# Another order inside the last attention layer, and additions of gathered rows placed one at a time

## The chip, the cores and the metric

The kernel runs on one core of a Trainium2 chip. The metric is device time in microseconds (us) of one execution, the median of several runs. Everything is float32.

## What is computed

The input is x of shape (8, 256, 32, 32): eight items, each with 256 channels and 1024 tokens. There are two layers. The first is attention with 8 heads of 64 whose softmax runs over the query axis. The second normalises the tokens, does attention without heads, whose keys and values are the normalised tokens themselves, adds it to its input, normalises again and adds a mixture of experts: 8 experts, of which every token uses the best two.

```python
def _L1_attn_ref(x, W):
    xa = jnp.einsum('bnd,ed->bne', x, W)
    scores = jnp.einsum('bne,bme->bnm', xa, x)
    attn = jax.nn.softmax(scores, axis=-1)
    return jnp.einsum('bnm,bmd->bnd', attn, x)

# _L1_ffn_ref: logits = tokens @ router_w.T; the two largest of 8; combine = their
# normalised weights;  out = tokens + sum over e of
#     combine[:, e:e+1] * (gelu(tokens @ w1[e] + b1[e], approximate=False) @ w2[e] + b2[e])

x = _L0_conv_ref(x, w_qkv, b_qkv, w_out, b_out)          # layer 0
t = _to_tokens(x)
t = t + _L1_attn_ref(_ln_t(t), L1_attn_W)                # attend
t = t + _L1_ffn_ref(_ln_t(t), router_w, w1, b1, w2, b2)  # norm 2, experts
x = _from_tokens(t, x)
```

## The kernel before

The items are worked one after the other. For each of items 0 to 6 the kernel does layer 0 (`layer0`, lines 465 to 676), the attention of layer 1 (`attend`, line 678), the second norm and the router's logits (`normed`, line 996), stores the tokens with their norm added (`sums`), and sends every token's row to the lists of its two experts (`dispatch`). Matmuls of the next item's values (`pv`, line 408) are placed as filling into `attend` by the calls `fill(place)`. After layer 0 of item 7, `experts` (line 1226) works through the lists of items 0 to 6 in blocks of 256 rows and writes the results to `y` in the chip's memory. Last come `attend` and `dense` (line 1458) for item 7: `dense` does all 8 experts for all tokens of item 7, in 16 half steps (expert e, half n) of 512 tokens. In the same time the class `Results` (line 1336) finishes items 0 to 6.

**Attention of layer 1.** The normalised tokens are transposed (`pt_n`, line 281), multiplied by W (`px`, line 708), and the scores come from a scheme of seven products on sums of halves instead of eight. One `Pair` k makes two blocks of 128 queries: products into the banks x and v of one `ps1` tile and into `ps1z` (line 761). ACT copies x away after the first, the s2 and the s3 product (lines 744, 754 and 756), and VectorE adds the other banks to these copies and takes the row's minimum on the way (`nlow`, line 771). `rest` adds two last products, finds the maximum, and ACT takes the exponential (lines 795, 804, 812). A block of weights must then be turned before its product with the values (`mix`: the eight matmuls of one `py` group, line 861, and the eviction t, line 870). Blocks 0 and 7 are turned by TensorE (`turn_now`, tile `pa`). Blocks 1 to 6 are turned by VectorE in squares of 32 (`turn`, line 833), and their 16 pieces are then moved by ACT copies and by transfers of SP's queue, half and half (line 844; both appear in the profile as spare<-home, aT<-home or home<-home). The program's order is written out by hand, in the last lines of `attend`, and with `tc.issue_after`, which places an instruction behind another on its engine. PSUM has three two-bank tiles (`big`: ps1, pa, px, pt_n) and two one-bank tiles (`acc`: ps1z, py, pdy).

**Results.** A unit is a block of 128 tokens of one item; there are 56. For a unit, POOL gathers the two rows of every token from `y` (`yk`, line 1391: two gathers of 128 KB), and VectorE adds them, with their weights, to the item's sums `o` (line 1413: two instructions). SP loads one item's sums ahead (1 MB, `load`). When an item's eight units are done, it is stored in two halves: VectorE transposes a half (`oT`, line 1449), and SP sends four transfers of 128 KB (line 1456). The calls `tick(place, instruction)` in `attend` and `dense` look the place up in the table `PLACES`, which says how many units are added behind that instruction, how many are gathered and how many halves are stored. The gathered rows have eight slots.

**Dense stage.** A half step has `hidden` (eight matmuls `pdh`, line 1518, and the activation on ACT) and `collect` (two `pdy` banks of eight matmuls each, line 1542, each emptied by two VectorE instructions, line 1551). `hidden` of one half step is issued ahead of `collect` of the one before. `tick(("dense", k), ...)` comes once for each half step, after its second bank.

**Last norm.** For item 7 the second norm of blocks 0 to 6 is done ahead of the last `py` group (`fill("last products")`), that of block 7 after it; all write one tile `n2`. POOL adds the norm to the tokens in one instruction (line 1008).

## Time and profile before

| | us |
|---|---|
| median of three runs (lowest, highest) | 2337.22 (2333.23, 2338.61) |
| the profiled execution: own time | 2328.95 |
| the profiled execution: span | 2327.1 |
| attention of item 6, first transpose to last py (next item's values in it) | 71.8 |
| attention of item 7, the same | 86.9 |
| end of it to the router's first matmul | 10.4 |
| from there to the end of TensorE's work | 125.6 |
| from there to the end of the span | 7.3 |

The profile shows one execution. Its time and its span differ by 1.9 us, which lie around the span. A row of a stretch or a group gives busy time, the number of instructions in brackets, and for groups the mean duration of one and the idle time of the engine before them, with what ended it. In a list of waits, the numbers are the total, how many times, and the longest.

### The profile page before, as it was taken

To read this page: it belongs to the slowest core of one execution; us is meant where nothing else is said; L and a number is where in the kernel's file an instruction comes from. 1 tells how busy PE (TensorE), PEld (TensorE's weight loads), DVE (VectorE), ACT (ScalarE), POOL (GpSimd) and SP (SyncE) were. 2 spreads that over 40 slices of the span, in tenths; PEclk is the share of its full clock that TensorE was granted. 3 is DMA by queue.
4 is the path that set the end of the run, shared out by engine and by line. 5 is a ranking of instruction groups with operands and counts; after the bars stand their busy time and mean duration, and the time that the engine had idled before them with its cause. 6 is when DMAs were issued, how large, how long until landed. Compare 5 with 4: busy or idle time off the path is not lost.

```text
span 2327.1 us, 37989 instructions
## 1 busy us (share of the span) xinstructions
PE 2261.6 (97%) x13059; PEld 1216.1 (52%) x13059; DVE 1554.5 (67%) x4029; ACT 1163.0 (50%) x2138; POOL 410.7 (18%) x392
## 2 busy tenths in 40 slices
PE   9999999999999999999999999999999999998798
PEld 3345533563456335643564355435553488884565
DVE  5775687567855786578657775777568766436655
ACT  3664466456635663656365646465646622225211
POOL 0000012000200020003000200020002135545563
PEclk9999999999999999999999999999999999999899
DMA  8995201020103010201020101100111157765574
GB/s 294 385 386 154 68 17 39 9 56 13 44 2 62 8 49 1 46 19 53 3 46 19 49 8 29 36 26 13 23 42 42 49 145 192 192 199 145 154 210 113
DMA packets 278759, 200.10 MB, mean 86 GB/s; under 512 B 189576, under 2 KB 232232, under 8 KB 276776
## 3 DMA queue, kind: packets, MB, share of 16 engines
q1 hardware_dynamic: 252472, 139.14, 21.2%
q0 software_dynamic: 25008, 58.01, 7.8%
q8 instruction: 104, 1.70, 0.3%
q10 hardware_dynamic: 1088, 0.52, 0.1%
q14 instruction: 87, 0.71, 0.1%
HBM read 108.88 MB, written 110.90 MB: 94 GB/s over the span
## 4 chain that ended last, share of the span: by engine, by line
PE 80%; ACT 5%; DVE 4%; issue 4%; DMA 3%; POOL 3%; SPq 1%; another core or an unknown queue 0%; DVEq 0%; ACTq 0%; POOLq 0%
PE po L569 19%; PE psc L492 19%; PE py L861 7%; PE pqk L371 7%; PE pr L671 5%; PE pv L408 4%; PE ps L761 4%; PE ph L1269 3%; PE pe L1295 3%; PE px L708 2%; POOL yk L1391 2%; PE pqk L349 2%; PE ps1z L761 2%; DMA y<-yb 1%; ACT aT L844 1%
## 5 line engine op out<-in xcount | busy, mean ns | idle before, releaser
L533 ACT ACTIVATE ex<-psc,nmax 128x1024 f32<-128x1024 f32 x512 | 570.0, 1114 | 299.8 <-DVE scrap L516 217.4
L492 PE MATMUL psc<-qk,qk 64*64 64x512 f32 x4096 | 575.8, 593 | 3.8 <-ACT ex L533 3.5
L569 PE MATMUL po<-ex,vs 64*64 64x512 f32 x4096 | 570.6, 591 | 3.6 <-DVE vs L549 2.6
L516 DVE TENSOR_SCALAR_CACHE_REDUCE scrap<-psc,nmax 128x512 f32<-128x512 f32 x512 | 384.2, 750 | 160.3 <-PE psc L492 133.6
L507 DVE TENSOR_REDUCE nmax<-psc 128x1 f32<-128x512 f32 x512 | 350.1, 684 | 9.3 <-PE psc L492 9.3
L492 PEld LDWEIGHTS psc<-qk,qk 64*64 64x64 f32 x4096 | 180.4, 132 | 279.2 <-ACT ex L533 132.6
L569 PEld LDWEIGHTS po<-ex,vs 64*64 64x64 f32 x4096 | 176.5, 132 | 275.6 <-DVE vs L549 82.1
L1081 POOL DMA_INDIRECT rows<-n,d_at x112 | 109.0, 973 | 661.1 <-DVE nmax L507 660.8
L1008 POOL TENSOR_TENSOR t<-t,n 128x2048 f32<-128x2048 f32 x8 | 36.3, 4535 | 875.5 <-DVE n L263 875.5
L371 PE MATMUL pqk<-xT,wqkv 128*128 128x512 f32 x384 | 171.2, 599 | 0.0
L861 PE MATMUL py<-n,spare 128*128 128x256 f32 x512 | 122.0, 394 | 11.3 <-DMA out_dram<-oT 3.8
L336 ACT ACTIVATE qk<-pqk,b_qks 128x512 f32<-128x512 f32 x124 | 85.6, 690 | 86.7 <-PE pqk L371 77.6
L1391 POOL DMA_INDIRECT yk<-y,yat x112 | 111.3, 994 | 76.4 <-issue 28.4
L371 PEld LDWEIGHTS pqk<-xT,wqkv 128*128 128x128 f32 x384 | 71.0, 190 | 99.9 <-issue 77.0
L408 PE MATMUL pv<-wqkv,xT 128*128 128x512 f32 x256 | 121.5, 599 | 1.5 <-DVE v L416 1.0
L861 PEld LDWEIGHTS py<-n,spare 128*128 128x128 f32 x512 | 100.7, 198 | 38.1 <-issue 23.9
L671 PE MATMUL pr<-wo,res 128*128 128x256 f32 x512 | 111.9, 379 | 0.7 <-ACT res L588 0.7
L844 ACT COPY spare<-home 32x256 f32<-32x256 f32 x256 | 103.0, 402 | 10.0 <-DVE home L833 6.7
L671 PEld LDWEIGHTS pr<-wo,res 128*128 128x128 f32 x512 | 97.2, 190 | 17.7 <-ACT res L588 4.7
L1279 ACT ACTIVATE hb<-ph,wb 128x256 f32<-128x256 f32 x96 | 40.1, 470 | 126.9 <-issue 89.4
L533 ACT ACTIVATION_READ_ACCUMULATOR ex<-psc,nmax 128x1 f32 x512 | 99.1, 194 | 0.0
L870 DVE SCALAR_TENSOR_TENSOR t<-py,rs,t 128x256 f32<-128x256 f32 x64 | 30.5, 476 | 98.0 <-PE py L861 85.3
(256 smaller groups left out, 2939.7 us busy)
## 6 DMA issues: line engine op xcount, KB each, us to landing
rows<-wb SPq DMA_DIRECT2D x7, 8192.0 KB
xr<-rows SPq DMA_DIRECT2D x252, 64.0 KB
y<-yb POOLq DMA_DIRECT2D x63, 256.0 KB
xs<-in_x_dram SPq DMA_DIRECT2D x64, 128.0 KB
spare<-home SPq DMA_DIRECT2D x256, 32.0 KB
out_dram<-oT SPq DMA_DIRECT2D x60, 128.0 KB
xT<-in_x_dram SPq DMA_DIRECT2D x7, 1024.0 KB
sums<-t SPq DMA_DIRECT2D x7, 1024.0 KB
```

The source lines that it names most:

```text
L371: mm = nc.tensor.matmul(pq[:, ts(n, 512)], wqkv[:, cc, t, ts(g, P)], xT[:, cc, ts(n, 512)], start=(cc == 0), stop=(cc == NCC - 1),)
L408: nc.tensor.matmul(pv, self.xT[:, cc, ts(i, P)], wqkv[:, cc, 2, :], start=(cc == 0), stop=(cc == NCC - 1),)
L492: mm = nc.tensor.matmul(pss[at, h][ts(c, DK), ts(n, 512)], k[r, j * P + c * DK : j * P + (c + 1) * DK], q[r, ts(n, 512)], start=True, stop ...
L507: firsts[at, h] = nc.vector.tensor_reduce(nmax, pss[at, h][:, ts(0, 512)], AX.X, ALU.max, negate=True)
L516: seconds[h] = nc.vector.tensor_scalar(scrap, pss[at, h][:, ts(1, 512)], -1.0, nmaxes[at, h], ALU.mult, ALU.min, accum_out=nmax,)
L533: nc.scalar.activation(ex, pss.pop((at, h)), AF.Exp, bias=nmaxes.pop((at, h)), scale=1.0, accum_out=sums[at][:, h : h + 1],)
L569: mm = nc.tensor.matmul(po[n][ts(h, DK), :], vss[at][keys, h, :], exps[at, h][keys, ts(n, 512)], start=(j == 0 and turn == 0), stop=(j == ...
L671: nc.tensor.matmul(pr[:, :C], res[:, g, ts(i, P)], wo[:, g, :], start=(g == 0), stop=(g == NPAIR - 1))
L761: return nc.tensor.matmul(to, stationary[:, ts(self.k, P)], moving, start=start, stop=True, skip_group_check=not start,)
L844: move(to[ts(k, SQ), a], since[ts(a, SQ), k])
L861: evicted["mixed"] = nc.tensor.matmul(py[:, :D], aT[m], n1[:, m, :], start=(m == 0), stop=(m == NT - 1))
L1391: ins = nc.gpsimd.indirect_dma_start(out=self.slot(at)[:, k, :], out_offset=None, in_=self.group.y[:, :], in_offset=bass.IndirectOffsetOnAxis(
```

## The change

It has five parts.

- **Order of the attention, for all items.** `Pair.middle` is split: `middle` has the s2 product, `end` has the s3 product. In pair 2 the value projection (`fill("between")`) stands between them, in pair 3 the product py of block 2's weights (`mix(*third)`). `fill("last products")` no longer issues a value projection, so their number stays the same. In pair 3 the ACT copy of the first product and the product into `ps1z` are issued in a separate step (`open`), after pair 2's copies of turned pieces. The exponential of block 2 is issued later (`soften`), behind the first copy of pair 2.
- **The last transposition.** Of block 6's 16 pieces, ACT copies 10 and SP transfers 6.
- **Where rows are added.** `PLACES` puts 14 units into the attention of item 7 and 42 into the dense stage, three for each half step: one behind the first bank's eviction, two behind the second's. Before, 22 were in the attention (three behind most py evictions), 3 at the gates and 31 in the dense stage. All stores of items 0 to 6 now stand in the dense stage, one half of an item for each half step; four of them were in the attention. Each gather follows an addition.
- **Twelve slots.** Eight as before, and four in the buffers of the experts' rows (`xr`). Twelve units are gathered at the start of item 7's attention, two before.
- **Last norm of item 7 in two tiles.** Blocks 0 to 6 and block 7 have tiles of their own, and POOL's addition becomes two.

```diff
...
 
         return t.unsqueeze(2).to_broadcast([P, NT, n])
 
+    class Split:
+
+        def __init__(self, first, last):
+            self.first, self.last = first, last
+
+        def __getitem__(self, key):
+            p, i, c = key
+            return self.first[p, i, c] if i < NT - 1 else self.last[p, 0, c]
+
     class Norm:
 
 
...
             elif place == "norm 2":
                 with tc.issue_after(evicted["mixed"].ins):
                     self.project(True)
-            self.values(1)
+            if place != "last products":
+                self.values(1)
 
         def all(self):
             for _ in range(3):
...
             def __init__(self, k):
                 self.k = k
                 both = big(f"ps1_{b}_{k}")
-                self.x, v = both[:, :HALF], both[:, HALF:]
-                self.z = acc(f"ps1z_{b}_{k}")
+                self.x, self.v = both[:, :HALF], both[:, HALF:]
                 self.ex = [homes[EX[2 * k + h]] for h in range(2)]
                 self.low = [
                     small.tile([P, 1], F32, tag=f"nlow{h}", name=f"nlow_{b}_{k}_{h}")
...
                 ]
                 self.left = self.ex[0][:, :HALF]
                 self.product(self.x, a11, b11, True)
+                if k < 3:
+                    self.open()
+                else:
+                    self.product(self.v, a12, b21, True)
+
+            def open(self):
                 self.first = nc.scalar.copy(self.left, self.x)
-                second = self.product(v, a12, b21, True)
-                tc.declare_no_dep(second.ins, self.first.ins, reason="the other bank")
+                if self.k < 3:
+                    second = self.product(self.v, a12, b21, True)
+                    tc.declare_no_dep(second.ins, self.first.ins, reason="the other bank")
+                self.z = acc(f"ps1z_{b}_{self.k}")
                 self.product(self.z, s1_, t1_, True)
-                self.add(self.left, v, 3.0e38, self.low[0])
+                self.add(self.left, self.v, 3.0e38, self.low[0])
 
             def middle(self, behind=None):
+                with tc.issue_after(behind.ins) if behind else nullcontext():
+                    mm = self.product(self.x, s2_, t2_, False)
+                self.second = nc.scalar.copy(self.ex[0][:, HALF:], self.x)
+                return mm
+
+            def end(self):
                 far = self.ex[1][:, HALF:]
-                with tc.issue_after(behind.ins) if behind else nullcontext():
-                    self.product(self.x, s2_, t2_, False)
-                self.second = nc.scalar.copy(self.ex[0][:, HALF:], self.x)
                 self.product(self.x, s3_, t3_, False)
                 self.third = nc.scalar.copy(far, self.x)
-                self.add(far, self.z, 3.0e38, self.low[1])
+                tick(("low", self.k), self.add(far, self.z, 3.0e38, self.low[1]))
                 return self
 
             def product(self, to, stationary, moving, start):
...
 
                 def even():
                     tick(("max", 2 * k), self.add(ex0[:, HALF:], self.z, self.low[0], nmax[0]))
+                    if k != 1:
+                        self.soften()
+
+                def soften():
                     with tc.issue_after(behind.ins) if behind else nullcontext():
                         nc.scalar.activation(
                             ex0, ex0, AF.Exp, bias=nmax[0], scale=-1.0, accum_out=ssum[0][:, 0:1]
                         )
 
+                self.soften = soften
                 def odd():
                     last = nc.vector.tensor_scalar(
                         scrap, self.x, -1.0, self.low[1], ALU.mult, ALU.min, accum_out=nmax[1]
...
 
             at_sq, at_aT = SQ_AT[i]
             sq = homes[at_sq]
-            nc.vector.transpose(sq, ex)
+            tick(("squares", i), nc.vector.transpose(sq, ex))
             if at_aT is None:
                 aT = two.tile([P, S], F32, tag="tr", name=f"aT_{b}_{i}")
             else:
...
             since = sq.rearrange("p (m k q) -> p k m q", k=NQ, q=SQ)
             for a in range(NQ):
                 for k in range(NQ):
-                    move = nc.sync.dma_start if (a + k) % 2 else nc.scalar.copy
+                    away = (a + k) % 2 and (i < 6 or a > 0)
+                    move = nc.sync.dma_start if away else nc.scalar.copy
                     with tc.issue_after(behind[a * 2 // NQ].ins) if behind else nullcontext():
                         move(to[ts(k, SQ), a], since[ts(a, SQ), k])
             return [aT[:, ts(m, P)] for m in range(NT)]
...
             for m in range(NT):
                 nc.tensor.transpose(pt[:, ts(m, P)], ex[:, ts(m, P)], ident)
             aT = two.tile([P, S], F32, tag="tr", name=f"aT_{b}_{i}")
-            nc.vector.tensor_copy(aT, pt)
+            tick(("now", i), nc.vector.tensor_copy(aT, pt))
             return [aT[:, ts(m, P)] for m in range(NT)]
 
         def mix(at, aT, ssum, more):
...
         def turned(at, ex, ssum, more, behind=None):
             return at, turn(at, ex, behind), ssum, more
 
-        pairs = [Pair(0).middle(), Pair(1).middle()]
+        pairs = [Pair(0)]
+        pairs[0].middle()
+        pairs[0].end()
+        pairs.append(Pair(1))
+        pairs[1].middle()
+        pairs[1].end()
         first, second = pairs[0].rest(pairs[1].third)
         second = turned(*second)
         third, fourth = pairs[1].rest()
         now = turn_now(0, first[1])
         pairs.append(Pair(2))
+        pairs[1].soften()
+        pairs.append(Pair(3))
         mix(0, now, *first[2:])
-        pairs[2].middle(evicted["mixed"])
+        between = pairs[2].middle(evicted["mixed"])
+        with tc.issue_after(between.ins):
+            fill("between")
+        pairs[2].end()
         third = turned(*third, (pairs[2].first, pairs[2].second))
         fourth = turned(*fourth, (pairs[2].second, pairs[2].second))
         mix(*second)
         fifth, sixth = pairs[2].rest()
-        pairs.append(Pair(3))
-        mix(*third)
-        pairs[3].middle()
+        pairs[3].open()
+        between = pairs[3].middle()
+        with tc.issue_after(between.ins):
+            mix(*third)
+        pairs[3].end()
         fifth = turned(*fifth, (pairs[3].second, pairs[3].second))
         sixth = turned(*sixth, (pairs[3].third, pairs[3].third))
         mix(*fourth)
...
             tick("normed", layer_norm(t2, n2, 1e-5, f"f{b}"))
         else:
             n2 = norm.dst
-            tick("normed", norm.blocks(NT - 1, NT))
+            written = norm.blocks(NT - 1, NT)
+            tick("normed", written)
         fill("norm 2")
         nT = one.tile([P, NCC, S], F32, tag="nT", name=f"n2T_{b}")
         tick("turned", to_channels(n2, nT, f"n2_{b}"))
 
-        nc.gpsimd.tensor_add(t2, t2, n2)
+        if norm is None:
+            nc.gpsimd.tensor_add(t2, t2, n2)
+        else:
+            for part, at in ((n2.first, slice(0, NT - 1)), (n2.last, slice(NT - 1, NT))):
+                added = nc.gpsimd.tensor_add(t2[:, at], t2[:, at], part)
+                tc.add_manual_dep(added.ins, written.ins.name, BEHIND)
         fill("normed 2")
         l = logits(b, nT)
         return n2, nT, l
...
 
 
 
-        SLOTS = 8
+        EXTRA = 4
+        SLOTS = 8 + EXTRA
         PLACES = {
-            **{("xa", ec): (0, 1, 0) for ec in range(2)},
-            ("max", 0): (0, 1, 0),
-            **{("max", i): (0, 1, 0) for i in range(1, 8)},
-            ("mixed", 0): (4, 2, 0),
-            **{("mixed", i): (3, 2, 1 if i > 2 else 0) for i in range(1, 7)},
-            "gates": (3, 3, 0),
-            ("dense", 0): (1, 3, 2),
-            ("dense", 1): (3, 2, 0),
-            **{("dense", k): (3 - k % 2, 3 - k % 2, 1) for k in range(2, 10)},
-            ("dense", 10): (3, 2, 1),
-            ("dense", 11): (2, 0, 1),
-            ("dense", 12): (3, 0, 2),
-            ("dense", 13): (0, 0, 2),
+            ("now", 0): (2, 0),
+            ("mixed", 0): (2, 0),
+            ("low", 2): (1, 0),
+            ("squares", 5): (1, 0),
+            ("low", 3): (1, 0),
+            ("max", 6): (1, 0),
+            ("max", 7): (1, 0),
+            ("mixed", 4): (3, 0),
+            ("now", 7): (2, 0),
+            ("dense", 0, 0): (1, 0),
+            ("dense", 0, 1): (2, 0),
+            ("dense", 1, 0): (1, 0),
+            ("dense", 1, 1): (2, 1),
+            **{("dense", k, 0): (1, 1) for k in range(2, NT + 6)},
+            **{("dense", k, 1): (2, 0) for k in range(2, NT + 6)},
+            ("dense", NT + 6, 0): (0, 1),
         }
 
         def __init__(self, group):
             self.group = group
             self.units = [(b, i) for b in group.items for i in range(NT)]
-            self.yks = [
-                two.tile([P, self.SLOTS // 2, 2, D], F32, tag="xT", name=f"yk_{n}")
-                for n in range(2)
+            tiles = [
+                two.tile([P, 4, 2, D], F32, tag="xT", name=f"yk_{n}") for n in range(2)
             ]
+            self.slots = [t[:, i] for i in range(4) for t in tiles]
+            for n in range(self.EXTRA):
+                self.slots.append(rowp.tile([P, 2, D], F32, tag="xr", name=f"yx_{n}"))
             self.sent, self.added = 0, 0
             self.pairs, self.totals = [], []
             self.whole = []
 
         def slot(self, at):
-            return self.yks[at // (self.SLOTS // 2) % 2][:, at % (self.SLOTS // 2)]
+            return self.slots[at % self.SLOTS]
 
...
-        def gather(self, behind=None):
+        def gather(self):
             at = self.sent
             if at == len(self.units):
                 return
...
             self.sent += 1
             b, i = self.units[at]
             for k in range(2):
-                ins = nc.gpsimd.indirect_dma_start(
+                nc.gpsimd.indirect_dma_start(
                     out=self.slot(at)[:, k, :],
                     out_offset=None,
                     in_=self.group.y[:, :],
...
                         ap=self.group.kept[b][1][k][:, i : i + 1], axis=0
                     ),
                 )
-                if behind is not None:
-                    tc.add_manual_dep(ins.ins, behind.ins.name, BEHIND)
...
                 )
             if i == 1 and n + 1 < len(self.group.items):
                 self.load(n + 1, added)
-            if i == NT - 1:
-                self.whole += [(b, total, n) for n in range(NH2)]
+            if i % NB == NB - 1:
+                self.whole.append((b, total, i // NB))
 
         def begin(self):
             self.load(0)
-            for _ in range(2):
+            for _ in range(self.SLOTS):
                 self.gather()
 
         def tick(self, place, behind=None):
-            added, sent, stored = self.PLACES.get(place, (0, 0, 0))
             if place == ("max", 0):
                 self.scored = behind
+            added, stored = self.PLACES.get(place, (0, 0))
             if added:
                 with tc.issue_after(behind.ins):
                     for _ in range(added):
                         self.add()
-            for _ in range(sent):
-                self.gather(behind)
+                        self.gather()
             for _ in range(stored):
                 if self.whole:
                     b, total, n = self.whole.pop(0)
-                    store(b, total, n)
+                    with tc.issue_after(behind.ins):
+                        store(b, total, n)
 
     def store(b, total, n):
 
...
                         ALU.mult,
                         ALU.add,
                     )
-            tick(("dense", e * NH2 + n), added)
+                tick(("dense", e * NH2 + n, i // 2), added)
             if n == NH2 - 1 and e + NWB < E:
                 weights(e + NWB)
             if e == E - 1:
...
             nonlocal norm
             others.tick(place)
             if place == "last products":
-                norm = Norm(t1, one.tile([P, NT, D], F32, tag="xa", name=f"n2_{b}"), 1e-5, f"f{b}")
+                n2 = Split(
+                    one.tile([P, NT - 1, D], F32, tag="xa", name=f"n2_{b}"),
+                    two.tile([P, 1, D], F32, tag="yb", name=f"n2_last_{b}"),
+                )
+                norm = Norm(t1, n2, 1e-5, f"f{b}")
                 return norm.blocks(0, NT - 1)
```

## The prediction

> **What bounds the kernel now.** I read the page's busy rows and chain first, then the table of stretches, then the groups and waits of the stretches that differ.
>
> ```profile
> PE 2261.6 (97%) x13059; PEld 1216.1 (52%) x13059; DVE 1554.5 (67%) x4029; ACT 1163.0 (50%) x2138; POOL 410.7 (18%) x392
> ...
> PE 80%; ACT 5%; DVE 4%; issue 4%; DMA 3%; POOL 3%; SPq 1%; another core or an unknown queue 0%; DVEq 0%; ACTq 0%; POOLq 0%
> ```
>
> TensorE is busy nearly everywhere, and 80% of the chain that ended last is TensorE work. The change removes no matmul, so it can win only the time in which TensorE waits or runs at a lower clock. The stretches show where that is:
>
> ```profile
> core 0: us, PE busy (x) PEld busy (x) DVE busy (x) ACT busy (x) POOL busy (x), PEclk, DMA share, GB/s
> 1630.00:1702.00 72.00, 69.12 (x246) 42.81 (x245) 39.96 (x93) 40.41 (x89) 0.00 (x0) 1.00 0.22 37
> 2097.00:2184.00 87.00, 72.30 (x233) 45.18 (x231) 55.34 (x124) 40.62 (x89) 51.02 (x52) 0.90 0.63 168
> 2160.00:2168.00 8.00, 3.26 (x15) 2.21 (x14) 6.61 (x16) 6.68 (x15) 6.17 (x7) 0.81 1.09 290
> 2184.00:2195.00 11.00, 4.96 (x24) 2.65 (x24) 9.71 (x28) 0.41 (x2) 4.39 (x3) 0.72 0.60 156
> 2225.00:2290.00 65.00, 63.18 (x218) 40.79 (x216) 38.88 (x84) 10.12 (x16) 43.69 (x44) 1.00 0.69 204
> ```
>
> The first two rows are the same attention, of item 6 and of item 7. Item 6 needs 72 us (5.2 of them for the next item's values) at clock 1.00; item 7, with the gathered rows of the other items beside it, needs 87 at 0.90. Without gaps the matmuls of one attention come to about 62.0 us (transposes 1.73, px 6.87, 28 products at 0.86, two turned tiles 1.74, eight py groups at 3.45). So item 7 loses 25 us. The groups of the two stretches name part of it (item 7 first, then item 6):
>
> ```profile
> L861 PE MATMUL py<-n,spare 128*128 128x256 f32 x64 | 20.4, 491 | 6.0 <-DMA out_dram<-oT 3.8 <-issue 2.2
> ```
> ```profile
> L861 PE MATMUL py<-n,spare 128*128 128x256 f32 x64 | 14.5, 380 | 1.5 <-DMA spare<-home 1.5
> ```
>
> The same 64 matmuls take 491 ns instead of 380 and wait 6.0 us instead of 1.5. In item 7 the matmul that waits is shown behind a store: the stores of finished rows lie ahead of the transposing copies in the same SP queue. The waits of 2095 to 2196 us give the others, the last norm's among them:
>
> ```profile
> DVE t L870 <- remote: 12.7, 2, 8.0
> ...
> PE pt_n L281 <- DVE n L263: 5.1, 2, 3.5
> ...
> PE py L861 <- DMA out_dram<-oT: 3.8, 1, 3.8
> ...
> PE ps L761 <- ACT home L756: 2.8, 1, 2.8
> ```
>
> **What the Trainium skill says.** "Trainium Kernel Development and Optimization", Key Constraints: transfers from the SP, ACT and POOL queues share the same 16 engines and interleave. The trace agrees: in 2160 to 2168 us, with gathers, stores and transposing copies at once, the DMA share is 1.09, and eight spare<-home copies take 8.95 us from issue to the last landing, against 5.2 in items before. "TensorE: Matmul & The Clock Gate", Part 1: the clock falls after an idle window of some 3.4 us and returns after as long a busy one. The trace shows the fall (0.73 after the 3.8 us wait, 0.72 in the last norm), but also 0.89 and 0.83 before any wait so long; I take from it only that slow matmuls follow waits. "Perfetto Trace Analysis", Identifying Performance Opportunities: stages with different limits may gain by interleaving. Here the dense stage has TensorE bound and VectorE with room (38.88 of 65 us), the attention has not.
>
> **Part 1, attention order, items 0 to 6.** Matmuls only change places: the value projection pv_2 goes whole between the third and fourth product of pair 2, py_1 between those of pair 3. In items 1 to 5 the gaps before are 0.19, 0.33 and 0.73 us in the middle and 0.65 to 0.91 before py_3; each costs 0.27 more than its label, since the first matmul pair after it takes about 1.12 instead of 0.86. I followed the new order by hand with the trace's durations: the middle gaps change places (0.86 before the fourth product of pair 2, 1.06 before pair 3's ps1z) and come to about +0.1. Before py_3 the last transposition now has 10 ACT copies and 6 transfers instead of 8 and 8; SP spaces its transfers by 0.65 us, so the last lands 1.3 us earlier, and the ACT copies end only 0.8 later and earlier than that. The gap goes: −1.03 in each (mean 0.76, and 0.27), −1.74 in item 6 (1.47 there). Item 0 has other neighbours and loses about 1.0. Sum: 5 × (−1.03 + 0.1) − 1.74 + 0.1 + 1.0, about **−5.3**. That nlow_3_0 now stands behind an eviction on VectorE, and home_4 ahead of an exponential on ACT, is in that walk. Their bounds: +1 in each of seven items if the moved copy delays its next product, −1.5 if the middle gaps vanish: **−10 to +5**.
>
> **Part 2, attention order and placing, item 7.** Before, 22 units (of 56) are added here on VectorE, in threes behind the evictions, with four stores (1.24 us of transpose and four transfers of 128 KB each). After, it is 14 units in ones, twos and one three, and no store. A unit is two additions of 0.41 us back to back. So VectorE loses 8 × 0.82 + 4 × 1.24 = 11.5 us of work, and SP 16 transfers. Gathers are 26 units by the end of this stage either way; now 24 gathers go at once at the start (POOL 1.26 us each, about 30 us, done near 2127, before the first transposing copies at about 2140), the rest one unit per addition. POOL waits there with nothing else behind it but the next gathers. The loss of 25 us by terms:
> - Wait behind the stores (3.84) and the issue wait after it (2.17): −6.0. Next late are the ACT copies, which end within 0.5 us of the matmul.
> - Slowed py groups, 4.40 + 5.30 + 6.15 + 5.38 against 3.45 each: 7.4. The two stalls they follow go, but 2.8 us before the fourth product of pair 2 and 2.35 before that of pair 3 stay; I take back 2 and keep −5.4.
> - The gaps by order (0.85, 1.05, 0.68, 2.32, 2.78, 0.85; together 8.5): about 6.5 stay, −2.0.
> - Smaller slow matmuls and gap tails: −1.1.
> Sum **−14.5**: py_7 ends near 2169 instead of 2183.8, before the gain of part 1. Bounds: −18 (no clock loss) and −4 (only the store wait goes, and 2 us of new gaps come).
>
> **Part 3, last norm in two tiles.** From the end of py_7 to the router's first matmul it is 10.4 us now (2183.8 to 2194.21). VectorE does three units and a store before the statistics (3 × 0.82 + 1.24 = 3.7) and a transpose before the last block (1.2). After, two units and no store stand there, and they come before py_6 already. The two banks of the transposes and the tile of its own let the last block pass without waiting for the others. By the same durations 6.0 us remain: **−4.4**, bounds −6 and 0. POOL's addition, one of 4.50 us, becomes two of together about as long (by size 3.94 and 0.56). Its reader is the biases' addition on VectorE about 15 us later, so it costs nothing; gathers queue behind it, but twelve units lie ready.
>
> **Part 4, dense stage.** It takes 31 units before (3 more at the gates), 42 after, three in each half step of 6.89 us, and one store. VectorE's work per half step: 4 evictions (0.475) + 6 additions (0.41 to 0.479) + 1.24, together 5.6 to 6.0 us: 81 to 87% full. Followed by hand, the second eviction ends 2.5 us after its product and its bank is wanted 5.3 us after it; the cover is 2.8 us. POOL needs 7.55 us for three units, 0.66 more than a half step, but 12 lie ready and only 30 are gathered here, so the store of rows loses about 1.3 units in all. If a cover failed, it would show as TensorE waiting for t<-pdy; I take **0**, bounds −3 (the two waits of 1.67 and 1.87 us at 2268 and 2292 go) and +8. The last stores now stand 1.5 half steps (10 us) ahead of the end; the tail of 7.3 us stays, at most +2.
>
> **Sum.** −5.3 − 14.5 − 4.4 + 0 = −24.2, against the profiled execution's 2328.95: 2304.7. That execution stands 8.3 below the median of the three runs, so the forecast for a median is **2313**.
>
> **Rivals.**
> - *Half the gain.* The share of 1.09 came from gathers and copies as much as from stores; then the transposing copies stay late. For it: 26 units are gathered in this stage as before, and the 1 MB loads of o stay. Against: 24 of the gathers end before the copies start. Part 2 gives −5, part 3 −2, part 1 −3: −10, about 2327.
> - *Slower: VectorE becomes the bound of the dense stage.* The 3 units, store and evictions reach 6.0 of 6.89 us by the longer addition; if contention for memory or late gathers stretch an addition from 0.48 to over 0.63, a half step exceeds 6.89, VectorE falls behind and TensorE waits for its two banks. At 0.9 us an addition it is 8.5 us a half step, and 14 × 1.6 = +22; with −15 from the rest, +7: 2344. For it: VectorE already waits 12.3 us for something "remote" there. Against: in 2225 to 2290 it is 60% busy with only a half unit less per half step.
> - *Order worse everywhere.* The moved copies delay products in items 0 to 6: +7 instead of −5.3, and 2325 with the rest kept; with part 2 halved, 2335, no change.
> - *Not done.* The instruction order of the queues is as described, so that the change does nothing gets no chance of its own.
>
> **How the numbers follow.** Forecast 0.6; half the gain 0.2; order worse 0.1 (half of it no change); slower 0.1. About 0.2%, 4.7 us, is what a measurement here can tell. Faster 0.82, same 0.06, slower 0.12. The forecast's own range, from the bounds, is 2302 to 2324; with half the gain and the order rival added, 2301 to 2334, which leaves out under 2 in 10.
>
> **What would show it.** Right: item 7's stretch about 72 us with its clock over 0.95; no py waiting behind out_dram<-oT; py groups at about 380 ns; py_7 to router near 6 us; dense stage unchanged within 2 us; gap before py_3 gone in items 1 to 6. Wrong: t<-pdy late and pdy waiting for it, additions waiting for yk, an item of attention longer than before, or DMA share still at 1 beside spare<-home.

## The result and the profile after

The changed kernel is slower: 2346.65 us median of six runs against 2333.97 of six of the kernel before, ratio 1.0049 (95% interval 1.0039 to 1.0060), where 2313 was forecast. Measured again twice, on the chip of the third and fourth groups of experiments, it was 1.0050 (1.0033 to 1.0066) and 1.0042 (1.0027 to 1.0057).

By stage, worked out from the two traces (starts and ends of TensorE's groups, us):

| | before | after | difference | forecast |
|---|---|---|---|---|
| start of item 7's attention | 2096.9 | 2096.5 | −0.4 | −5.3 |
| item 7's attention | 87.0 | 90.2 | +3.2 | −14.5 |
| its end to the router's first matmul | 10.3 | 7.3 | −3.0 | −4.4 |
| from there to TensorE's last matmul | 125.6 | 137.6 | +12.0 | 0 |
| from there to the span's end | 7.3 | 13.0 | +5.7 | 0 to +2 |
| span | 2327.1 | 2344.5 | +17.4 | −24.2 |

The profiled execution of the kernel before took 2328.95 us, less than any of its six timed runs, so the spans differ by more than the medians (12.7).

Page and stretches of the changed kernel, the same rows as before and one more:

```profile
PE 2260.8 (96%) x13059; PEld 1217.1 (52%) x13059; DVE 1555.9 (66%) x4029; ACT 1171.0 (50%) x2154; POOL 409.0 (17%) x393
...
PE 82%; ACT 5%; DVE 5%; DMA 3%; SPq 2%; issue 2%; another core or an unknown queue 1%; POOL 0%; DVEq 0%; ACTq 0%; POOLq 0%
```
```profile
core 0: us, PE busy (x) PEld busy (x) DVE busy (x) ACT busy (x) POOL busy (x), PEclk, DMA share, GB/s
1630.00:1702.00 72.00, 69.78 (x247) 43.30 (x247) 40.79 (x95) 41.70 (x92) 0.00 (x0) 1.00 0.22 36
2097.00:2184.00 87.00, 66.20 (x218) 40.47 (x217) 45.27 (x105) 41.48 (x91) 46.87 (x49) 0.90 0.48 129
2160.00:2168.00 8.00, 7.06 (x27) 5.11 (x28) 6.85 (x15) 6.63 (x18) 2.86 (x3) 1.00 0.25 55
2170.00:2175.00 5.00, 4.46 (x24) 3.44 (x23) 2.66 (x8) 4.92 (x14) 3.27 (x4) 1.00 0.70 151
...
2225.00:2290.00 65.00, 54.54 (x173) 35.40 (x173) 36.90 (x76) 9.24 (x15) 41.29 (x43) 0.91 0.72 215
```

The stretch of 2160 to 2168 us can't be compared with the same stretch before. Other work stands in it now, the pieces home<-home of an earlier block, and the DMA share of 0.25 is theirs. SP issues the pieces of the last two blocks (spare<-home) from 2168.6 to 2177.7 us. There the forecast holds: the share is at most 0.70 where it was 1.09, the clock is 1.00, and SP issues all 14 in 9.1 us, where the last eight alone needed 8.95 beside the stores. (The prediction calls these 8.95 us the time to the last landing; the line it comes from shows only the time of SP's queue.)

Yet TensorE is busy for 66.2 us of the 87, less than before (72.3), and in the dense stage for 54.5 of 65 (63.2 before), where VectorE also works less (36.9, 38.9 before). Something makes both wait. The groups of the attention show that the slow py matmuls behind a store are gone (380 ns, no wait), and that one wait has come in another place:

```profile
L887 PE MATMUL py<-n,spare 128*128 128x256 f32 x64 | 14.5, 380 | 0.0
L887 PE MATMUL py<-n,aT 128*128 128x256 f32 x48 | 13.9, 455 | 11.9 <-DVE aT L879 11.9
```

The waits of 2095 to 2196 us say who was waited for (total, times, longest):

```profile
PE py L887 <- DVE aT L879: 11.9, 1, 11.9
...
DVE aT L879 <- remote: 8.8, 1, 8.8
...
ACT home L759 <- remote: 5.6, 1, 5.6
```

VectorE's copy aT<-pa reads eight transposes, which by the profile end at 2123.96. It starts at 2138.03, and in the same instant (2138.07) ACT starts home<-ps, which reads a product that ended at 2124.8. There is one core, so "remote" is no other core. By the semaphore records of the trace, both wait for one semaphore alone, TensorE's (a semaphore is the counter by which one engine tells another that it is done). It steps at 2138.01, 2138.05 and 2138.09 us, for three products whose shown ends are 2123.96, 2124.82 and 2125.68. So three products with 0.86 us between their shown ends are told of within 0.08 us: the signals came late and in a bunch, the first 14 us after the shown end. The Trainium skill ("Perfetto Trace Analysis", Per-instruction lifecycle) says that a matmul's end in a profile is an estimate and that the way of its signal is not shown; here that unseen part is what costs. VectorE's signals pass at the same time: ACT's copy aT<-home, which waits for VectorE alone, starts at 2129.18, 0.03 us after the transposition that it reads has ended. In order of time, POOL beside it:

```profile
start us, us, engine line op out<-in xcount [idle before <-releaser]
2102.84 1.27 POOL L1441 DMA_INDIRECT yk<-y,yat  x1 [2.08 <-DMA y<-yb]
2104.41 1.01 POOL L1441 DMA_INDIRECT yk<-y,yat  x1 [0.30 <-issue]
...
2132.46 0.95 POOL L1441 DMA_INDIRECT yx<-y,yat  x1 [0.30 <-issue]
2139.92 0.95 POOL L1441 DMA_INDIRECT yk<-y,yat  x1 [6.50 <-DVE o L1461]
```

The 24 gathers of the start run back to back, one each 1.26 us, to 2133.4. TensorE's signal comes 4.6 us later. The dense stage repeats it: trains of 14, 12, 16 and 12 gathers end at 2239.9, 2258.7, 2282.8 and 2302.3, and TensorE's gaps (3.53, 3.03, 3.90 and 0.44 us) end at 2243.2, 2261.9, 2286.4 and 2305.4. Its waits:

```profile
ACT dh L1575 <- remote: 34.8, 3, 15.3
...
DVE t L1599 <- remote: 18.0, 4, 7.8
...
PE pdy L1590 <- DVE t L1599: 10.9, 4, 3.9
```

POOL itself then stops for want of slots, since the additions stand behind the held evictions (it waits 33.5 us for them in this stage); a new train starts when they go on. The kernel before has such waits too (t<-remote, 12.7 us in the list shown before the result), and trains of 2 to 16 gathers.

VectorE at the end, in order of time:

```profile
2330.25 1.23 DVE L1497 STREAM_TRANSPOSE oT<-o 128x1024 f32<-128x1024 f32 x1
2331.41 1.22 DVE L1599 SCALAR_TENSOR_TENSOR t<-pdy,all_gates,t 128x256 f32<-128x256 f32 x3
2332.55 1.23 DVE L1497 STREAM_TRANSPOSE oT<-o 128x1024 f32<-128x1024 f32 x1
2335.61 1.25 DVE L1497 STREAM_TRANSPOSE oT<-t 128x1024 f32<-128x1024 f32 x1 [1.83 <-DMA out_dram<-oT]
2337.78 1.25 DVE L1497 STREAM_TRANSPOSE oT<-t 128x1024 f32<-128x1024 f32 x1 [0.92 <-DMA out_dram<-oT]
```

Two stores of item 6 come among the last evictions, and item 7's own stores wait for the two oT buffers. Before, the last oT<-t started at 2320.73, 0.9 us after TensorE's last matmul; now it is 6.2 us after it.

### The profile page after: what moved, and what is told of

It is laid out like the page before. It is cut to its first block, busy times and chain, and to the rows that moved or that the text cites. A ratio compares the mean times of both kernels' runs of the same rounds, so it can differ in the third digit from the quotient of the medians.

```text
span 2344.5 us, 38025 instructions
## 1 busy us (share of the span) xinstructions
PE 2260.8 (96%) x13059; PEld 1217.1 (52%) x13059; DVE 1555.9 (66%) x4029; ACT 1171.0 (50%) x2154; POOL 409.0 (17%) x393
## 4 chain that ended last, share of the span: by engine, by line
PE 82%; ACT 5%; DVE 5%; DMA 3%; SPq 2%; issue 2%; another core or an unknown queue 1%; POOL 0%; DVEq 0%; ACTq 0%; POOLq 0%
PE po L579 19%; PE psc L502 19%; PE pqk L380 7%; PE py L887 7%; PE pr L681 5%; PE pv L417 4%; PE ps L781 4%; PE ph L1313 3%; PE pe L1339 3%; PE px L718 2%; PE pdy L1590 2%; PE pqk L358 2%; PE pdh L1566 2%; SPq L870 2%; PE ps1z L781 1%
## 5 line engine op out<-in xcount | busy, mean ns | idle before, releaser
L870 ACT COPY spare<-home 32x256 f32<-32x256 f32 x272 | 109.4, 402 | 16.9 <-DVE home L858 11.9
L887 PE MATMUL py<-n,spare 128*128 128x256 f32 x512 | 115.5, 380 | 0.2 <-issue 0.2
L887 PE MATMUL py<-n,aT 128*128 128x256 f32 x384 | 90.6, 391 | 11.9 <-DVE aT L879 11.9
L1313 PE MATMUL ph<-xb,wb 128*128 128x256 f32 x384 | 91.6, 382 | 4.7 <-DMA wb<-wpack,w_at 4.6
```

The source lines that it names most:

```text
L870: move(to[ts(k, SQ), a], since[ts(a, SQ), k])
L887: evicted["mixed"] = nc.tensor.matmul(py[:, :D], aT[m], n1[:, m, :], start=(m == 0), stop=(m == NT - 1))
L1313: last = nc.tensor.matmul(ph[:, ts(fc, BR)], wb[:, dc * FF + fc * P : dc * FF + (fc + 1) * P], xb[:, dc, :], start=(dc == 0), stop=(dc == ...
```

## Experiments

**Theory 1:** gathers issued back to back by POOL hold back TensorE's signals. **Theory 2:** the new placing overloads VectorE beside the dense stage. **Theory 3:** the attention order loses. Ratios are to the kernel before on the same chip, with 95% intervals. The experiments ran on four chips; the kernel before took 2330 to 2333 us on three of them and 2316 on one. Groups three and four had the same chip; other times are compared within a group.

### First group: which part, and which kind of transfer (before: 2333.4)

e1_order: the change, with `Results` and its table as before.

```diff
-        EXTRA = 4 ... PLACES of the change, 12 slots
+        SLOTS = 8 ... PLACES, gather(behind), tick as before
```


> The changed attention order, 10/6 transposition and two-tile norm, with the additions, gathers, stores and eight slots placed as before the change. Theory 1 (back-to-back trains of indirect gathers on POOL hold back the completion signals of TensorE, and the change lengthened these trains): within 4 us of the kernel before, 2330 to 2338, since the gathers come in trains of 4 to 16 as before. Theory 2 (the new placing overloads VectorE in the dense stage): also near before. Theory 3 (the attention order itself is what lost): about 2344 to 2348, as the changed kernel.

2333.65 us, 0.9994 (0.9983 to 1.0004). e2_places: the kernel before, with the changed `Results`.

```diff
-        SLOTS = 8 ...
+        EXTRA = 4 ... PLACES and tick of the change
```


> The attention order, transposition and norm as before the change, with the changed placing of additions, gathers and stores and twelve slots. Theory 1: slower than before by 9 to 15 us, 2343 to 2349, with a gap of some 10 us of TensorE in item 7 that ends when the first 24 gathers are through. Theory 2: slower too, but with the loss in the dense stage alone and no such gap. Theory 3: as before, 2334.

2347.01 us, 1.0063 (1.0046 to 1.0080), with a gap of 13.8 us before the first py group. So the loss is the placing's; the order does no harm (item 7's attention starts 2.2 us earlier in e1_order's trace) but gains little. Theory 3 falls.

e3_paced:

```diff
         def begin(self):
-            for _ in range(self.SLOTS):
+            for _ in range(2):
                 self.gather()
+        # ten more, one behind each of ("xa", 0..1) and ("max", 0..7)
```


> The changed kernel, but two units instead of twelve are gathered at the start of item 7's attention, and the other ten one by one behind ten instructions of that attention (as many are gathered by its end). Theory 1: the gap of 11.9 us before the first py group goes, the dense stage stays as in the changed kernel: 2334 to 2340. Theory 2 and 3, and also the view that the bytes of the gathers are what hurts: 2344 to 2349, unchanged.

2345.42 us, 1.0045 (1.0028 to 1.0062). It tests nothing: with twelve slots free, the gathers behind the first additions waited for no addition, and the trace shows the same 24 back to back (2100.8 to 2131.6) and a gap of 14.0 us.

e4_plain:

```diff
-                nc.gpsimd.indirect_dma_start(out=self.slot(at)[:, k, :], ...)
+                row = (2 * at + k) * P
+                nc.sync.dma_start(self.slot(at)[:, k, :], self.group.y[row : row + P, :])
```


> The changed kernel, with each indirect gather of 128 rows by POOL replaced by a plain transfer of 128 consecutive rows of y by SP's queue, so that the rows are not those of the tokens; bytes, slots and places are the same, and POOL issues nothing here. Theory 1: no wait of VectorE or ACT for something remote is left, TensorE's gaps of 11.9 us in the attention and of 3 to 4 us in the dense stage go: 2312 to 2325. The view that bytes and transfers beside the stage are what hurts, and theory 2: TensorE's gaps stay, 2340 to 2350.

2326.78 us, 0.9969 (0.9957 to 0.9982), 20 us below e2_places, which has the same placing. No wait for something remote is left from 2095 us to the end, at a DMA share of 0.82 in 2225 to 2290 us (0.72 with gathers). The bytes are therefore not what holds the signals. The edit changes two things at once, though, who issues the transfers and that their rows lie scattered, and it doesn't tell which of them counts. TensorE still has gaps of 14.5 us in the attention, shown behind ACT, VectorE and spare<-home: SP's queue now carries 112 transfers more. That may be why it missed 2312 to 2325; it was not tested.

### Second group: pauses and slots (before: 2316.5)

e5_pause, and e7_order_pause (on e1_order) and e8_before_pause (on the kernel before) with the same edit:

```diff
             for k in range(2):
+                with tc.issue_after(self.rested.ins) if self.rested else nullcontext():
                     ins = nc.gpsimd.indirect_dma_start(...)
+                with tc.issue_after(ins.ins):
+                    self.rested = nc.gpsimd.memset(rest_a_while, 0.0)   # 128 x 384
```


> The changed kernel with a small clearing of 128x384 on POOL (by the size of others, some 0.4 us) after each gather: the same gathers in the same order, no longer back to back, POOL's period 1.7 to 2.0 us instead of 1.26. Theory 1 (back-to-back gathers hold back the signals): the gap of 11.9 us and those of 3 to 4 us in the dense stage shrink to under a half, 2328 to 2338. Rival (it is the number of gathers in flight or their bytes, not their rate; POOL is only slower with the clearings): 2345 to 2352.

> The changed attention order and norm with the old placing (as the first experiment), with the same clearing after each gather. Theory 1: gathers' trains cost that kernel too (gaps of 2.5, 2.3, 4.1 and 4.0 us); 2318 to 2328, faster than before by 6 to 15 us. Rival: 2333 or slower, as POOL's slower gathers come late.

> The kernel before with the same clearing after each gather, nothing else. Theory 1: gaps of 2.8, 3.8 and 2.2 us in item 7's attention shrink, 2320 to 2330. Rival: 2334 or slower.

e5_pause 2312.53 (0.9983, 0.9974 to 0.9993), e7_order_pause 2321.77 (1.0022, 1.0014 to 1.0029), e8_before_pause 2322.64 (1.0026, 1.0015 to 1.0037). No engine waits for anything remote in any of them. In the last two the last norm is late instead (17 us from the last py to the router, where it was 10 to 14): with eight slots and slower gathers the additions ahead of it come late (VectorE waits 4.5 and 4.9 us for gathered rows there).

The expected times were written for a chip on which the kernel before takes 2334 us. e7_order_pause and e8_before_pause fell into their ranges only because this chip is faster, which is luck: both were expected to be faster than the kernel before and are 5 and 6 us slower. e5_pause lies below its range for the same reason. What e8_before_pause does show is item 7's attention: 78.6 us, with no wait for anything remote, where the kernel before took 87.0 on another chip.

e6_slots4:

```diff
-        EXTRA = 4
-        SLOTS = 8 + EXTRA
+        EXTRA = 0
+        SLOTS = 4
```


> The changed kernel with 4 slots instead of 12, nothing else: no train can be longer than 8 gathers (10 us), since POOL then waits for an addition. Theory 1: no gap over 3 us before the first py group; dense gaps shorter; 2332 to 2340. Rival (many slots help and the placing is what costs): additions wait for their gathers, 2348 to 2360.

2318.77 us, 1.0009 (1.0000 to 1.0018), no remote wait, although 70 gathers ran back to back from 2203.6 to 2294.1. That could be the slots or the chip, so this group couldn't judge theory 1.

### Third group: the same, on a chip where before takes 2329.9

e9_after and e10_before are the two kernels as they are; e5b_pause is e5_pause; e11_pause_early adds:

```diff
+            "gates": (3, 0),
-            ("dense", 0, 0): (1, 0), ... ("dense", NT + 6, 0): (0, 1),
+            **{("dense", k, 0): (1, 1) for k in range(NT + 5)},
+            **{("dense", k, 1): (2, 0) for k in range(NT + 5)},
+            ("dense", NT + 5, 0): (0, 1),
```


> The changed kernel itself, once more, on the chip of this call, where the kernel before may take another time than the 2334 us of the first comparison (it took 2316 in the last one). Theory 1: on a chip where trains of gathers hold no signals back, the changed kernel is within 0.2% of before or faster, its cost there being only its late last stores (+5); where they do, +12 as at first. Rival (the loss has nothing to do with held signals): +12 on any chip.

> The kernel before itself, for its trace on this chip: ratio 1.000. Theory 1: if it takes about 2316 us here, VectorE and ACT never wait for something remote for more than 3 us in item 7's attention and in the dense stage; if about 2334, they do.

> The changed kernel with the clearing after each gather, beside the two others on one chip. Theory 1: where the changed kernel has held signals, this is faster than it by 15 to 30 us, and at about 2312 on any chip; where it has none, within 3 us of it. Rival: at the changed kernel's time or slower.

> The same with the additions of the dense stage one half step earlier (three units at the gates, then three in each of half steps 0 to 12, the last store in 13), so that the last stores of item 6 come before the last transposes. It should end 4 to 6 us before the kernel with clearings alone (the tail after TensorE's end grew from 7.3 to 13.0 us by the change): about 2307. Rival: the tail comes from the queue of stores and stays; same time.

e9_after 2340.39 (1.0050, 1.0033 to 1.0066), e10_before 2329.30 (0.9994, 0.9982 to 1.0005), **e5b_pause 2312.79** (0.9927, 0.9901 to 0.9953), **e11_pause_early 2309.61** (0.9914, 0.9892 to 0.9937). e10_before waits up to 8.1 us for something remote, as theory 1 expected of a chip with this time. e9_after's +10.5 us fits theory 1 and its rival alike. But a clearing after each gather, which adds work, takes 27.6 us away. The paused kernel takes the same time on both chips (2312.5, 2312.8), the kernel before doesn't (2316.5, 2329.9). Stretches of e5b_pause:

```profile
2097.00:2184.00 87.00, 77.09 (x284) 45.83 (x283) 58.98 (x144) 45.94 (x99) 75.42 (x107) 0.98 0.53 143
...
2225.00:2290.00 65.00, 65.00 (x229) 43.16 (x228) 45.01 (x98) 12.67 (x20) 58.37 (x81) 1.00 0.75 226
```

TensorE is busy for all 65 us, with VectorE at 45.0 and POOL at 58.4 us, both busier than in the changed kernel (36.9 and 41.3). That ends theory 2. e11_pause_early's tail is 9.5 us (12.4 in e5b_pause). The medians differ by 3.2 us, less than the 4 to 6 expected, and the intervals of the two overlap. That the late stores are a loss of their own rests on the tails in the traces. The kernel beats both others of this comparison, before and after.

### Fourth group: how the loss divides (before: 2329.6)

The clearing only for the 24 gathers of the start (e12_pause_begin), only for the others (e13_pause_rest), the early placing without clearings (e14_early), and the changed kernel (e15_after):

```diff
+                if at < self.SLOTS:        # e12;  at >= self.SLOTS in e13
                     self.rested = nc.gpsimd.memset(rest_a_while, 0.0)
```


> The changed kernel with the clearing only after the 24 gathers of the start. Theory 1: the gap of 11 us before the first py group goes and item 7's attention ends 8 to 12 us earlier than in the changed kernel on this chip; the dense stage keeps its gaps of 2 to 4 us: 8 to 12 us faster than the changed kernel. Rival (the held signals of the dense stage are all that counts, the gap is given back later): within 3 us of it.

> The changed kernel with the clearing after the other 88 gathers, the first 24 back to back. Theory 1: the gap of 11 us stays; the dense stage's gaps (10.9 us in the first trace) and the slow clock after them go: 10 to 18 us faster than the changed kernel on this chip. Rival: no faster, as the gathers come later.

> The changed kernel, no clearing, with the additions of the dense stage half a step to a step earlier, so that item 6's last stores come before the last transpositions. Theory 1 takes the late stores for a loss of its own: 3 to 6 us faster than the changed kernel, tail after TensorE's end about 8 us instead of 13. Rival: no difference.

> The changed kernel on the chip of this call, as the measure for the other three: 2340 to 2347 where signals are held, and about 2318 on a chip like that of the second call, where I expect no gap over 4 us in item 7's attention.

e15_after 2340.16 (1.0042, 1.0027 to 1.0057), e12_pause_begin 2336.79 (1.0028, 1.0016 to 1.0040), e13_pause_rest 2327.30 (0.9993, 0.9985 to 1.0000), e14_early 2337.89 (1.0039, 1.0030 to 1.0048). Against e15_after that is −3.4, −12.9 and −2.3, and only the second lies clear of the noise. It was as expected (−10 to −18): TensorE's work in the dense stage takes 121.5 us, where it takes 133.2 in e15_after. The other two missed: e12_pause_begin was expected at −8 to −12 and came near its rival's 3, e14_early at −3 to −6, though its tail did fall, from 12.8 to 9.4 us. So the dense stage is the larger part. With the start paced, the gap of 11 us goes, yet item 7's attention ends no earlier (2187.7 us, 2187.2 in e15_after): the next gathers form a train of 13 (2139.7 to 2155.7), and the wait returns behind it. In the stretch of 2140 to 2196 us:

```profile
DVE t L897 <- remote: 18.7, 3, 8.3
...
PE py L888 <- issue: 7.8, 2, 7.3
...
PE py L888 <- DVE t L897: 6.9, 1, 6.9
```

The parts are less than the whole: the two clearings one by one give 16.3 us, together, on the same chip, 27.6 below e9_after.

### Fifth group: chip, slots and length of the pause (before: 2331.0)

e16_slots4 is e6_slots4; e17_short is e11_pause_early with

```diff
-    rest_a_while = const.tile([P, 384], F32, name="rest_a_while")
+    rest_a_while = const.tile([P, 32], F32, name="rest_a_while")
```


> The kernel with 4 slots again. If it was the chip of the second call that held no signals back: here about 2330 to 2340, with waits of VectorE and ACT for something remote, above all beside the dense stage's long train. If few slots avoid it: 2316 to 2321 and no such wait on any chip.

> The kernel with clearings and earlier additions, the clearing 128x32 instead of 128x384 (some 0.15 us instead of 0.4). If what counts is that gathers aren't back to back in kind: about 2308 to 2311, as with the longer clearing. If the pause's length counts: part of the waits come back, 2315 to 2335.

e16_slots4 2339.81 (1.0034, 1.0022 to 1.0047), with these waits in 2095 to 2330 us:

```profile
ACT dh L1575 <- remote: 25.1, 3, 11.0
...
DVE t L1599 <- remote: 19.2, 4, 7.0
```

The same kernel that waited for nothing remote on the chip of the second group does so here; few slots don't avoid it. e17_short: 2342.18 (1.0056, 1.0034 to 1.0077), where e11_pause_early had 0.9914. That is more than the part of the waits that was expected back (2315 to 2335). POOL in order of time, e17_short and then e5b_pause:

```profile
2103.58 0.96 POOL L1441 DMA_INDIRECT yk<-y,yat  x1 [0.17 <-issue]
2104.54 0.14 POOL L1450 MEMSET rest_a_while<- 128x32 f32 x1
2104.85 0.96 POOL L1441 DMA_INDIRECT yk<-y,yat  x1 [0.16 <-issue]
```
```profile
2105.34 0.96 POOL L1444 DMA_INDIRECT yk<-y,yat  x1 [0.17 <-issue]
2106.30 0.43 POOL L1453 MEMSET rest_a_while<- 128x384 f32 x1
2106.90 0.96 POOL L1444 DMA_INDIRECT yk<-y,yat  x1 [0.16 <-issue]
```

The short clearing fits into the 0.30 us that lay between two gathers anyway: a gather each 1.27 us, as without it, and the waits are back (aT<-remote 15.9 us). The long one makes it 1.56 us (1.7 to 2.0 were expected), and they are gone. So it is the rate of the gathers that counts (or, not told apart from it, how many are under way at once), not what stands between them, with one reservation: the long clearing was run on the chip of the third group and the short one on this, though the waits are there on both without a clearing.

**What is shown and what is open.** Shown: on three of four chips, gathers at one each 1.26 us hold TensorE's signals back; at one each 1.56 us (run on one of these three) they don't, nor do plain transfers of the same bytes (run on another). Open: what in the chip delays these signals, whether POOL's issuing or the scattered rows do it, why the chip with 2316 us did not hold them, and where between 1.27 and 1.56 us the limit lies. Two runs are missing: the changed kernel unpaused on that chip, and the kernel before with clearings on a chip that holds signals.

## Why the prediction was wrong

- **Part 1 (−5.3; it was −0.4).** The mechanism held: no py group of items 1 to 6 waits any more for its turned pieces. The sizes didn't. By the prediction's own figures the middle gaps come to +0.4, not +0.1: before 0.19, 0.33 and 0.73 with 0.27 for each, 2.06; after 0.86 and 1.06 with 0.27 for each, 2.46. (In item 2 the new gaps are 0.80 and 1.07.) So items 1 to 5 gained 0.4 to 0.7 us each instead of 0.93, item 6 0.9 instead of 1.64, and item 0 lost 3.3 instead of 1.0 (1.7 in most other traces; in this one the clock fell there for 3.4 us).
- **Part 2 (−14.5; it was +3.2). Here and in part 4 the same step failed:** the gathers were priced by POOL's time alone, the 24 at the start with "nothing else behind it but the next gathers", and the bounds of −18 to −4 allowed no loss. What stood against it was in the quoted list: VectorE waiting 12.7 us for something remote, a wait with no term in the sum. Shown in its place: behind that train TensorE's signal comes 14 us late, and TensorE stands for 11.9 us. Under the clearings (e5b_pause) item 7's attention takes 70.3 us, where the sum had said 72.5. But the terms were right only in part. The kernel before with clearings (e8_before_pause), on the chip that held no signals, takes 78.6 us without any change of order or placing. So some 8 of the 14.5 us seem to have been held signals already. The wait behind the store still stands there, 3.5 us, and that term holds; but the 2.17 us after the store is gone, and the gap of 2.78 us, put down to the order, is 0.68.
- **Part 3 (−4.4; it was −3.0).** Right in kind, 1.4 us short: 7.3 us remain instead of 6.0.
- **Part 4 (0; it was +12.0, and the tail +5.7).** The covers were counted for VectorE's and POOL's time: 2.8 us for the second eviction, twelve units ready. (Its figures make the loss of rows in store 2.6 units, ten half steps of 0.66 us at 2.52 us a unit, not 1.3; the twelve ready units cover that too.) Neither failed, although TensorE did wait for t<-pdy, 10.9 us, which the prediction had named as the sign of a failed cover. With clearings, VectorE does the same additions and TensorE never stops in the stretch shown; the stage takes 124.6 us. What exceeded the cover is the late signal, which no busy time shows. The number of slots isn't the cause: with four instead of twelve the kernel is 8.8 us slower than before all the same (e16_slots4). The tail was mis-sized, 5.7 us and not at most 2. Earlier stores take back about 3 of it (e11_pause_early, e14_early); the rest stays open.
- **Rivals.** "VectorE becomes the bound" named 2344 and the right stage, but the wrong mechanism: its additions stayed at 0.48 us and it was less busy than before. It had the clue (12.3 us for something remote) as a point in favour and not as a mechanism. "Half the gain" and "order worse" didn't occur; e1_order shows the order to be neutral.
- **The sum.** With clearings and early stores the kernel reaches 2309.6 us where before takes 2329.9, −20.3 of the −24.2 forecast. That isn't the forecast come true behind one missing cost. On the chip that held no signals, the kernel before takes 2316.5 us and the paused changed kernel 2312.5, only 3.9 less. The work ahead of item 7 takes as long on both chips (its attention starts at 2097.6 us in e5_pause and in e5b_pause). So the 13 us by which the kernel before is slower on the other chip are most likely held signals of its own, which the forecast had put down to stores and order. This is not shown: there is no trace of the kernel before, as it is, from the chip that held none.

## What to carry to other kernels

A wait that the profile can give to no one, of an engine whose producer had ended long ago, is a cost with a mechanism of its own: price it before anything that could lengthen it, and before its loss is put down to something else. Where such waits end shortly after a train of gathers, try pacing the gathers; here 0.44 us of idle clearing after each was worth 1.2% of the whole time of the changed kernel. It isn't free: on the chip that held no signals, it made the kernel before 6 us slower. And compare both kernels on more than one chip before a cause is named.

## Not expected of the hardware

- TensorE's signals came up to 14 us after the shown end of a matmul, three of them within 0.08 us, and two waiters on different engines were released within 0.04 us.
- Chips differ in it: the kernel before took 2316.5 us on one and 2329.6 to 2333.4 on three others; the paused kernel took 2312.5 on the first and 2312.8 on one of the three.
- The Trainium skill ("TensorE: Matmul & The Clock Gate", Part 1) puts the fall of the clock after an idle window of some 3.4 us and its return after a busy one. The changed kernel's trace agrees: the clock was at half from 2131.7 to 2145.4 us, around the end of the gap of 2127.4 to 2139.3, and the matmuls of that time took 0.63 instead of 0.38 us. The kernel before doesn't: its clock was at half from 2130.7 to 2134.2, and the gaps in the 3.4 us ahead of that were only 1.05 and 0.68 us.
